# Attention scores of a transformer block: the first key tile of each unit in 64-key tiles of the array, the second in 128-key tiles

## The chip, the cores and the metric

The kernel runs on one core of one Trainium2 chip. The metric is the device time of an execution in microseconds (us). The engines named below are TensorE (PE; its weight loads are PEld in the profile), VectorE (DVE), ScalarE (ACT), GpSimd (POOL) and SyncE (SP), which here only starts transfers.

## The reference

A conditioned transformer block in float32, added to its own input. `x` is 4 x 1024 x 512, `cond_256` is 4 x 128, there are 16 heads of 32 features, and the feed-forward part has 2048 hidden features.

```python
def _tc_rmsnorm(x, t, gw, gb, bw, bb):
    g = (t @ gw.T + gb)[:, None, :]
    b = (t @ bw.T + bb)[:, None, :]
    inv_rms = jax.lax.rsqrt(jnp.mean(x * x, axis=-1, keepdims=True) + EPS)
    return g * x * inv_rms + b

def _attention(x, Wq, Wk, Wv, Wo):
    ...
    attn = jnp.einsum('blhd,bmhd->bhlm', q, k) / scale
    p = jax.nn.softmax(attn, axis=-1)
    o = jnp.einsum('bhlm,bmhd->blhd', p, v).reshape(B, L, D)
    return o @ Wo.T

def _swiglu(x, gate_w, hid_w, out_w):
    return jax.nn.silu(x @ gate_w.T) * (x @ hid_w.T) @ out_w.T

h = x + _attention(_tc_rmsnorm(x, t, g1w, g1b, b1w, b1b), Wq, Wk, Wv, Wo)
x = x + h + _swiglu(_tc_rmsnorm(h, t, g2w, g2b, b2w, b2b), gate_w, hid_w, out_w)
```

## The kernel before

Everything is kept with features on the 128 partitions and tokens in the columns. The 4096 tokens are 8 blocks of 512 (`NBLK`); a sequence is two blocks.

**Attention.** Its work is cut into `NR` = 256 units, numbered `r`. A unit is one block, one group of four heads (`HG`; 4 x 32 features fill the partitions), one half of 256 queries (`HQ`) and 256 of the 1024 keys, which are two key tiles of 128. Four units in a row (`UN`) go through all keys of one set of queries, called `j`. For a unit, `scores` (L307) takes keys as weights and queries as the moving data, one matmul for each head and key tile. A head's 32 features lie on 32 partitions, so each of these matmuls uses 32 rows of the array and 128 columns: the profile writes that as 32*128, and four heads are four tiles of the array that don't share rows. The result `sc` fills four of the eight PSUM banks, one bank for each head (two key tiles of 256 columns each), and there is one such buffer (`ps_sc`, L59). `keep` (L321) has ScalarE copy it to `raw` in SBUF. `running_max` takes the greatest score on VectorE; after the fourth unit `max_T`, `parts`, `parts_T` and `spread` turn the maximum into a shift for each query, laid out for all keys. `shifted` adds it on VectorE, `exponential` is ScalarE's, `weighted` (L374) multiplies the values by it on TensorE into `av`, and `accumulate` adds the exponentials of the four units with an accumulating DMA that GpSimd starts. `sums`, `inverse` and `normalize` finish a `j`.

**All other matmuls.** They go through `mm` (L109), which cuts a matmul's 128 output features into pieces of `columns[0]`: 32 in most of the program, giving 128*32 tiles, four of which share all rows and differ in columns. Transposes of the maximum (`mt`, L337) are 128*128, and some projections that follow them in the program's first part are too. A float32 matmul shows in the trace as two records of the matmul and two of the weight load; this is so on every line named here but the transposes.

**Order.** One hand-written loop over `g` (L774) sets the order of all engines but SP; nothing is reordered afterwards. In step `g` TensorE does `scores(g)`, later in the step `weighted` of unit `g` - 6, and between them the work of the feed-forward part or, before step `FS` = 60, the projections to keys, queries and values. The feed-forward products (`pa`, `pb`: a form of Strassen's product for gate and hidden; `pc`: the output product) fill the rest of each step from step 60 on; after step 268 they are alone. At `kind` 1 (every fourth step) `parts_T` stands ahead of the scores and `spread` behind them; otherwise `weighted` follows the scores directly. The loads are pinned to steps by a table.

Of the kernel before, what the change touches and what calls it, by code (L numbers as in the profile page):

```python
# [17 lines left out]
P = 128  # L18
# [6 lines left out]
def tile_cond_transformer_block(  # L25
# [13 lines left out]
    nc = tc.nc  # L39
# [267 lines left out]
    def scores(r: int):  # L307

        j, u = divmod(r, UN)
        m, qh = divmod(j, NB // HQ)  # L310
        keys, queries = kq[m, 0, u], kq[m, 1, qh]
        sc = ps_sc.tile([P, HG, 2, HQ], F32, tag="sc", name=f"sc{r}")
        for k in range(2):
            for i in range(HG):
                rows = slice(i * DH, (i + 1) * DH)
                nc.tensor.matmul(  # L316
                    sc[:, i, k, :], keys[rows, k * P : (k + 1) * P], queries[rows, :], start=True, stop=True
                )
        state["sc", r] = sc

    def keep(r: int):  # L321
# [382 lines left out]
    with tc.manual_schedule(  # L704
# [69 lines left out]
        while g < END:  # L774
# [16 lines left out]
            if g < NR:  # L791
                scores(g)
# [225 lines left out]
```

## Time and profile before

| | |
|---|---|
| median of 3 runs | 2432.27 us (2431.27 to 2441.08) |
| profiled execution, its own time | 2435.25 us |
| its span, first to last instruction | 2433.4 us |
| granted TensorE clock | 0.998 of full |
| scores (L316), matmul records | 4096, in 256 units |
| first and last start of a score matmul | 50.3 and 2088.5 us |

In the profile a group of instructions is named by its line, engine and operation and by what it writes and reads (`sc<-q,k`). The number behind x is the count of records. "128*32" ahead of a shape is the tile of the array that a matmul uses, rows by columns. Matmuls overlap, so a group's busy time is the time in which at least one of its records was running, and the mean length of one is longer than what it adds. What a block of matmuls costs is best read as the distance from its first start to the first start of what follows.

### The profile page before, as it was taken

To read this page: it belongs to the slowest core of one execution; us is meant where nothing else is said; L and a number is where in the kernel's file an instruction comes from. 1 tells how busy PE (TensorE), PEld (TensorE's weight loads), DVE (VectorE), ACT (ScalarE), POOL (GpSimd) and SP (SyncE) were. 2 spreads that over 40 slices of the span, in tenths; PEclk is the share of its full clock that TensorE was granted. 3 is DMA by queue.
4 is the path that set the end of the run, shared out by engine and by line. 5 is a ranking of instruction groups with operands and counts; after the bars stand their busy time and mean duration, and the time that the engine had idled before them with its cause. 6 is when DMAs were issued, how large, how long until landed. Compare 5 with 4: busy or idle time off the path is not lost. (4 is left out here: it accounts for less than half of the span.)

```text
span 2433.4 us, 72676 instructions
## 1 busy us (share of the span) xinstructions
PE 2378.9 (98%) x32553; PEld 1131.6 (47%) x32553; DVE 1938.6 (80%) x2183; ACT 1412.7 (58%) x1495; POOL 172.4 (7%) x207
## 2 busy tenths in 40 slices
PE   8999999999999999999999999999999999999999
PEld 3333334345454544545454545454545454434444
DVE  2688988888799988998899979997999799833322
ACT  3677777766566656755576657665666576512110
POOL 0000000000000000000000000000000000000000
PEclk9999999999999999999999999999999999999999
DMA  6599999988889788989888888898888889853442
GB/s 216 167 302 262 263 247 248 224 223 228 199 203 218 193 229 204 215 210 231 196 210 217 223 200 211 208 232 211 200 206 214 218 202 216 198 143 118 144 129 71
DMA packets 185988, 501.79 MB, mean 206 GB/s; under 512 B 21319, under 2 KB 78663, under 8 KB 158286
## 3 DMA queue, kind: packets, MB, share of 16 engines
q0 software_dynamic: 28656, 208.68, 44.3%
q1 hardware_dynamic: 156734, 288.47, 35.4%
q8 instruction: 256, 4.19, 0.7%
q14 instruction: 54, 0.44, 0.1%
q10 hardware_dynamic: 288, 0.01, 0.0%
HBM read 246.44 MB, written 41.97 MB: 119 GB/s over the span
## 5 line engine op out<-in xcount | busy, mean ns | idle before, releaser
L369 DVE TENSOR_TENSOR raw<-raw,shift 128x2048 f32<-128x2048 f32 (+1 forms) x320 | 588.8, 1856 | 26.1 <-ACT shift L364 26.1
L323 ACT COPY raw<-sc 128x2048 f32<-128x2048 f32 x256 | 479.6, 1873 | 181.6 <-PE sc L316 123.0
L372 ACT ACTIVATE raw<-raw 128x2048 f32<-128x2048 f32 x256 | 491.0, 1918 | 149.8 <-DVE raw L369 147.3
L328 DVE TENSOR_TENSOR rmax<-rmax,raw 128x1024 f32<-128x1024 f32 x384 | 469.5, 1223 | 47.5 <-ACT raw L323 41.2
L112 PE MATMUL pc<-h,ow 128*32 128x512 f32 x4096 | 469.1, 595 | 3.0 <-DMA ow<-in_out_w 2.1
L396 POOL DMA_DIRECT2D raw<-raw x192 | 165.3, 861 | 1944.9 <-ACT raw L372 864.3
L316 PE MATMUL sc<-q,k 32*128 32x256 f32 x4096 | 293.3, 400 | 1.1 <-ACT raw L323 1.1
L382 PE MATMUL av<-raw,v 128*32 128x256 f32 x4096 | 271.9, 383 | 21.6 <-ACT raw L372 21.1
L112 PE MATMUL pa<-x,fa 128*32 128x256 f32 x4096 | 269.9, 381 | 3.7 <-DVE pa L530 2.7
L112 PE MATMUL pa<-sums,fw 128*32 128x256 f32 x4096 | 267.9, 379 | 0.0
L112 PEld LDWEIGHTS pc<-h,ow 128*32 128x32 f32 x4096 | 128.3, 110 | 247.7 <-issue 226.6
L316 PEld LDWEIGHTS sc<-q,k 32*128 32x128 f32 x4096 | 184.9, 184 | 117.5 <-issue 74.9
L112 PE MATMUL pkq<-y,wkq 128*32 128x512 f32 (+1 forms) x1664 | 231.4, 594 | 4.3 <-ACT y L202 4.1
L112 PEld LDWEIGHTS pa<-x,fa 128*32 128x32 f32 x4096 | 123.4, 109 | 120.7 <-DVE pa L530 21.1
L112 PEld LDWEIGHTS pa<-sums,fw 128*32 128x32 f32 x4096 | 133.0, 110 | 88.0
L382 PEld LDWEIGHTS av<-raw,v 128*32 128x32 f32 x4096 | 110.4, 109 | 134.9 <-ACT raw L372 50.8
L583 DVE SCALAR_TENSOR_TENSOR res<-pc,res 128x512 f32<-128x512 f32 x128 | 88.2, 689 | 73.3 <-PE pc L112 70.4
L562 ACT ACTIVATE t<-pa 128x512 f32<-128x512 f32 x128 | 78.3, 611 | 109.9 <-PE pa L112 109.6
L545 ACT COPY pb<-pa 128x256 f32<-128x256 f32 x128 | 46.2, 361 | 164.3 <-PE pa L112 163.0
L112 PE MATMUL pb<-x,fw 128*32 128x256 f32 x2048 | 134.0, 379 | 1.2 <-ACT pb L545 1.2
L112 PE MATMUL pa<-x,fw 128*32 128x256 f32 x2048 | 134.0, 379 | 0.0
L112 PE MATMUL pb<-sums,fa 128*32 128x256 f32 x2048 | 133.9, 379 | 0.0
(108 smaller groups left out, 2163.9 us busy)
## 6 DMA issues: line engine op xcount, KB each, us to landing
raw<-raw POOLq DMA_DIRECT2D x192, 1024.0 KB, 9.2
fw<-sw SPq DMA_DIRECT2D x128, 512.0 KB, 7.1
fa<-in_gh_w SPq DMA_DIRECT2D x128, 384.0 KB, 6.1
ow<-in_out_w SPq DMA_DIRECT2D x128, 256.0 KB, 3.2
wkq<-in_kq_w SPq DMA_DIRECT2D x32, 512.0 KB, 6.3
v<-vs SPq DMA_DIRECT2D x128, 128.0 KB, 6.0
k<-kqs SPq DMA_DIRECT2D x124, 128.0 KB, 7.3
kqs<-st SPq DMA_DIRECT2D x61, 256.0 KB, 9.2
```

The lines of the kernel that those rows point to most:

```text
L112: nc.tensor.matmul(dst[k : k + n, :], w[:, k : k + n], moving, start=start, stop=stop, skip_group_check=seeded)
L316: nc.tensor.matmul(sc[:, i, k, :], keys[rows, k * P : (k + 1) * P], queries[rows, :], start=True, stop=True)
L323: nc.scalar.copy(raw[r].rearrange("p k h q -> p h k q"), state.pop(("sc", r)))
L328: nc.vector.tensor_tensor(rmax[j], rmax[j], raw[r][:, k, :, :], ALU.max)
L369: nc.vector.tensor_tensor(t, t, s.unsqueeze(1).to_broadcast(list(t.shape)), ALU.add)
L372: nc.scalar.activation(raw[r], raw[r], AF.Exp)
L382: nc.tensor.matmul(av[j][i * DH : (i + 1) * DH, :], v[m, u][:, k, i * DH : (i + 1) * DH], raw[r][:, k, i, :], start=(kt == 0), stop=(kt == ...
L396: nc.gpsimd.dma_start(out=acc[j].rearrange("p k h q -> p (k h q)"), in_=raw[r].rearrange("p k h q -> p (k h q)"), accum_op=ALU.add,)
L545: nc.scalar.copy(bank_b[p][:, RIGHT], bank_a[p][:, RIGHT])
L562: nc.scalar.activation(state["t", p], bank_a[p], AF.Tanh, scale=0.5)
L583: nc.vector.scalar_tensor_tensor(r, pp, 0.5, r, ALU.mult, ALU.add)
```

## The change

For the first key tile of each unit (`k` = 0), each head's matmul over 128 keys becomes two over 64 keys each, one behind the other: the first 64 keys go to partitions 0 to 63 of the head's bank, the other 64 to partitions 64 to 127. Each uses a tile of 32 rows and 64 columns of the array. The second key tile (`k` = 1) stays as it was, in tiles of 32 rows and 128 columns. Values written, their places and everything behind them are the same.

```diff
@@ -313,9 +313,16 @@
         for k in range(2):
             for i in range(HG):
                 rows = slice(i * DH, (i + 1) * DH)
-                nc.tensor.matmul(
-                    sc[:, i, k, :], keys[rows, k * P : (k + 1) * P], queries[rows, :], start=True, stop=True
-                )
+
+                wide = P // 2 if k == 0 else P
+                for part in range(0, P, wide):
+                    nc.tensor.matmul(
+                        sc[part : part + wide, i, k, :],
+                        keys[rows, k * P + part : k * P + part + wide],
+                        queries[rows, :],
+                        start=True,
+                        stop=True,
+                    )
         state["sc", r] = sc
```

## The prediction

> **What bounds the kernel now.** I read the page's first table, then the groups of instructions, then TensorE's records of the changed line, then a stretch of the timeline.
>
> The page's busy times and groups (busy us, mean ns of one | idle before and what ended it):
>
> ```profile
> PE 2378.9 (98%) x32553; PEld 1131.6 (47%) x32553; DVE 1938.6 (80%) x2183; ACT 1412.7 (58%) x1495; POOL 172.4 (7%) x207
> ...
> L323 ACT COPY raw<-sc 128x2048 f32<-128x2048 f32 x256 | 479.6, 1873 | 181.6 <-PE sc L316 123.0
> ...
> L316 PE MATMUL sc<-q,k 32*128 32x256 f32 x4096 | 293.3, 400 | 1.1 <-ACT raw L323 1.1
> L382 PE MATMUL av<-raw,v 128*32 128x256 f32 x4096 | 271.9, 383 | 21.6 <-ACT raw L372 21.1
> ```
>
> TensorE is busy 98% of the span; every other engine has room (VectorE 80%, ScalarE 58%). Only 54.5 us of the 2433.4 are free of matmuls. So time added to or taken from TensorE's stream of work moves the end almost one for one. The scores wait for nearly nothing (1.1 us in all 256 units). Their 2048 float32 matmuls appear as 4096 records: each is two passes over its 256 columns. Though scores and weighted values have equally many records of equal width, the scores take 293.3 us and the weighted values 271.9. The excess is the price of their other tiling (32*128, rows by columns of the array, amid 128*32), and the change is about nothing else.
>
> The records of the line (duration ns min/median/max):
>
> ```profile
> L316 PEld LDWEIGHTS sc<-q,k x4096: 181/184/185, 50.3 to 2088.3; 32*128 32x128 f32 x196
> L316 PE MATMUL sc<-q,k x4096: 374/374/478, 50.3 to 2088.5; 32*128 32x256 f32 x196
> ```
>
> Most records take 374 ns, the longest 478. In the trace these are the first four of a unit: they start with their own weight load and stand **104 ns** for it; later loads run behind matmuls.
>
> TensorE's timeline (start us, length us); compare starts, since ends are modelled and overlap:
>
> ```profile
> 1005.07 1.05 PE L112 MATMUL pa<-sums,fw 128*32 128x256 f32 x16
> 1005.93 1.05 PE L112 MATMUL pb<-sums,fa 128*32 128x256 f32 x16
> 1006.91 1.15 PE L316 MATMUL sc<-q,k 32*128 32x256 f32 x16
> 1007.99 1.07 PE L382 MATMUL av<-raw,v 128*32 128x256 f32 x16
> 1008.87 1.05 PE L112 MATMUL pa<-x,fa 128*32 128x256 f32 x16
> 1009.74 1.05 PE L112 MATMUL pa<-sums,fw 128*32 128x256 f32 x16
> 1010.60 0.61 PE L414 MATMUL sum<-raw,ones_sum 128*32 128x256 f32 x8
> 1011.14 1.09 PE L337 MATMUL mt<-ident,rmax 128*128 128x128 f32 x8
> ```
>
> Four things are to be seen. (1) Sixteen records inside one tiling take 1005.93 - 1005.07 = 0.86 us: four tiles at once, so four waves of **0.216 us**. (2) The same 16 records ahead of the scores take 0.98: changing the tiling costs **0.11 to 0.12 us**. (3) The scores last 1.08 from start to next start: 4 x 0.216 = 0.86, plus 0.104 for the exposed load, plus 0.11 for changing back. (4) From the sums to the transposes only the columns of the tile change, 32 to 128, with all rows kept, and it costs the same: 8 records, two waves or 0.43, take 1011.14 - 1010.60 = 0.54.
>
> **What the Trainium skill says.** "TensorEngine Tiling (Array Packing)", Key Properties: changing the tiling mode, not just the tile, drains TensorE. The trace agrees, at 0.11 us a time, also where only columns change. The same page, Available Configurations, lists 32x64 as eight independent tiles; no run here shows that mode. "TensorE: Matmul & The Clock Gate", LDWEIGHTS, says a load takes its columns divided by 1.2, in ns: 107 for 128, 53 for 64, 27 for 32. The trace agrees for 128 (104 exposed) and for 32 (the longest record of the weighted values is 404 against a median of 379: 25). The same page, Part 3, has 16 tiles split both ways running side by side; the trace of before has four at once, split one way.
>
> **The change part by part.** Per unit (there are 256):
>
> The first key tile was 4 matmuls of 32x128; it becomes 8 of 32x64, so 8 records become 16, each still 256 columns. They are 4 row groups by 2 halves. If all eight tiles run together, the array work stays two waves of 0.216: no gain, no loss. The weights hold the same number of columns.
>
> *Entering.* The stream still leaves 128*32, so that drain (0.11) stays. The exposed first load is of 64 columns: 53 ns by the skill, and 51 if I interpolate between the trace's 25 at 32 columns and 104 at 128. Saved: **-53**.
>
> *More starts.* Tiles start one after another, 7 ns apart in the records of the scores. Eight tiles end their starting 49 ns after the first instead of 21; the drain waits for the last. Added: **+28**.
>
> *The new switch in the middle.* Between the two key tiles the mode now goes from 32x64 to 32x128. I price it as in point 4, where only columns change: about 0.11 of drain. From the records' starts: the last start of one mode to the first of the next is 304 to 310 ns, against 196 within a mode, which makes **+112**. After it the first load of 128 columns has no matmul to hide behind, as now at entry: **+104**. This drain and this load did not exist, since the second tile's weights were loaded behind the first tile's matmuls.
>
> *Leaving.* From 32x128 to 128*32 as before: nothing.
>
> Sum: -53 + 28 + 112 + 104 = +191 ns a unit, times 256 = **+48.9 us**. The whole block, start to next start, goes from 1.08 to about 1.27 us.
>
> *What of it is hidden.* TensorE has waits that a later arrival would shorten: 21.1 us ahead of the weighted values (for ScalarE's exponential), 9 ahead of pa and 7 ahead of the sums where starts are later than in the undisturbed sequence. The waits ahead of weighted values number about 75 (by its weight loads), so at most 75 x 0.19 = 14 us can come back. But the copy of the scores, and the exponential queued behind it on ScalarE, also start later by what the scores lose, so I take about half or less: **-6**. Nothing else is reordered: no DMA, no wait and no buffer is added; the score banks are filled and emptied as before, ScalarE's copy waits 0.19 us longer and it has 42% idle. The program has 4096 more TensorE instructions (weights and matmuls, +6%); a unit's scores then have 24 record pairs in 1.27 us, 53 ns a pair, about the rate at which the whole stretch runs now (16 pairs in 0.86 is 54), so I price the issue at nothing. If this cover is gone, a first tile's 16 pairs at 54 ns take 0.86 instead of 0.43, +0.4 us a unit: the second rival below.
>
> Net +43 us. The profiled execution took 2435.25 us (span 2433.4, 1.85 around it), and the median of the runs is 2432.27, 3 lower. On the profile's time 2478, on the median **2475 us**.
>
> Bounds of what the trace does not show, the 32x64 mode: its drain may cost from 0 (the 64-to-128 change being no change of mode) to 0.12; its load exposed from 25 (no slower than 32 columns) to 104 (no faster than 128); the eight tiles from full overlap (0) to none between the halves (+0.43 a unit). The low end is a gain, hence the first rival.
>
> **The rivals.** *No drain in the middle (not slower).* Rows stay split by 32, and only the column limit moves; if TensorE lets the second tile's 128-column loads go into the background while the 64-wide matmuls run, the 112 and 104 fall away and -53 + 28 = -25 ns x 256 = -6 us: about 2426. The point that decides: if drain and exposed load in the middle are together under 72 ns instead of 216, a unit grows by less than 72 - 25 = 47 ns, and 256 x 47 ns = 12 us is the 0.5% named below. For it: the skill lists both as 4x row tilings. Against: the sums-to-transposes switch changes only columns and costs 0.11.
>
> *The halves don't overlap.* Both halves of a head lie in the same row group; in the program each matmul's two passes stand together. If a row group takes its work strictly in order, the second half's first pass starts only with the first half's second pass: one wave more, less the 28 of starts, so 191 + 188 = 379 ns x 256 = 97 us, less a little hidden: about 2525. If they don't overlap at all, two waves more: (191 - 28 + 432) x 256 = 152 us: about 2580. For it: no record of before has two tiles in one row group with split rows. Against: in 128*32 all four tiles share every row and run together, starting 3 to 7 ns apart.
>
> *The waits absorb it.* All 14 us of shortened waits come back, and a cheaper drain: +30, about 2462. This is the low side of my own case.
>
> **How the numbers follow.** Full overlap with a drain: 0.68, 2460 to 2490. Halves one wave apart: 0.11; not overlapping: 0.08. No drain: 0.11, within 0.5% but for a small part faster. A change of 0.5% (12 us) is about what a measurement of this kernel can tell from none. The range reaches from 2458 to 2540, through the one-wave rival; the no-drain and no-overlap ends, just under 2 in 10, are left out. Faster 0.04, same 0.09, slower 0.87.
>
> **What would show it.** The line of the scores should show 6144 records: 4096 of 32*64 with a longest of about 374 + 53 = 427 ns and 2048 of 32*128, whose first four a unit are still 478; weight loads near 135 ns for 64 columns. In the timeline the first key tile should last about 0.62 us, the second 0.64, the weighted values following at 1.27. A first tile of 0.83 or 1.03 means the halves wait for each other; a second one starting with 374 ns records means no drain. If the block grows by 0.19 us and the time by much less than 43, the waits ahead of the weighted values have shrunk; by much more, a queue behind the scores' copy has become late.

## The result and the profile after

The changed kernel takes 2465.01 us (median of 5 runs, 2464.53 to 2466.07) against 2433.89 before (5 runs): the ratio is 1.0121 with a 95% interval of 1.011 to 1.0132, so it is slower by about 31 us, clear of the spread of single runs (2431.27 to 2441.08 us before). The profiled execution took 2465.01 us with a span of 2463.2, 29.8 more than the span before, at the same granted clock of 0.998.

The page after, with the busy times and the groups of the scores, their copy and the weighted values (busy us, mean ns of one | idle before and what ended it; lines left out are marked):

```profile
PE 2421.6 (98%) x34601; PEld 1090.2 (44%) x34601; DVE 1940.6 (79%) x2183; ACT 1411.0 (57%) x1495; POOL 172.4 (7%) x207
...
L330 ACT COPY raw<-sc 128x2048 f32<-128x2048 f32 x256 | 479.6, 1873 | 210.7 <-PE sc L319 146.0
...
L319 PE MATMUL sc<-q,k 32*64 32x256 f32 (+1 forms) x6144 | 340.9, 409 | 0.2 <-ACT raw L330 0.2
...
L389 PE MATMUL av<-raw,v 128*32 128x256 f32 x4096 | 272.4, 384 | 15.3 <-ACT raw L379 15.0
```

TensorE is still at 98%, and VectorE and ScalarE are busy for the same time as before, to within 2 us. The scores' matmuls are busy for 47.6 us more (340.9 against 293.3). The span has grown by only 29.8 us, and one place where the difference went is in the last line: TensorE idles 15.0 us for ScalarE ahead of the weighted values, where it was 21.1.

The records of the scores' line after (duration ns min/median/max):

```profile
L319 PEld LDWEIGHTS sc<-q,k x6144: 127/131/185, 50.0 to 2122.4; 32*64 32x64 f32 x133, 32*128 32x128 f32 x66
L319 PE MATMUL sc<-q,k x6144: 373/400/479, 50.0 to 2122.6; 32*64 32x256 f32 x133, 32*128 32x256 f32 x66
```

The counts behind the forms are of a sample, two to one as they must be. In the single records, a weight load of 64 columns takes 127 to 133 ns. The first eight matmuls of a unit, of 64 columns, last 425 or 426 ns, 51 over the undisturbed 374; the first four of 128 columns last 478 or 479, as they did at the unit's entry before.

TensorE's timeline in the unit that was shown of before, unit 120 (start us, length us):

```profile
1021.39 1.05 PE L112 MATMUL pb<-sums,fa 128*32 128x256 f32 x16
1022.37 1.33 PE L319 MATMUL sc<-q,k 32*64 32x256 f32 x24
1023.63 1.07 PE L389 MATMUL av<-raw,v 128*32 128x256 f32 x16
1024.52 1.05 PE L112 MATMUL pa<-x,fa 128*32 128x256 f32 x16
```

The entry (1022.37 - 1021.39 = 0.98) and what follows are as before; the scores now last 1023.63 - 1022.37 = 1.26 us, and lasted 1.08. Inside them the single records have the first key tile for 617 ns from its first start to the first start of the second, and the second for 644 ns to the start of what follows. The first length holds in all 256 units to within 6 ns, the second wherever what follows doesn't wait. So the scores grew by 617 + 644 - 1076 = 185 ns a unit, 47.4 us in all; the span grew by 29.8.

### The profile page after: what moved, and what is told of

Its sections match the earlier page's. It is cut to its first block, busy times and chain, and to the rows that moved or that the text cites. A ratio compares the mean times of both kernels' runs of the same rounds, so it can differ in the third digit from the quotient of the medians.

```text
span 2463.2 us, 76771 instructions
## 1 busy us (share of the span) xinstructions
PE 2421.6 (98%) x34601; PEld 1090.2 (44%) x34601; DVE 1940.6 (79%) x2183; ACT 1411.0 (57%) x1495; POOL 172.4 (7%) x207
## 5 line engine op out<-in xcount | busy, mean ns | idle before, releaser
L319 PE MATMUL sc<-q,k 32*64 32x256 f32 (+1 forms) x6144 | 340.9, 409 | 0.2 <-ACT raw L330 0.2
L319 PEld LDWEIGHTS sc<-q,k 32*64 32x64 f32 (+1 forms) x6144 | 139.8, 147 | 209.3 <-issue 171.5
L371 ACT COPY shift<-sp 128x512 f32<-128x512 f32 x128 | 75.0, 586 | 106.5 <-PE sp L112 106.5
```

Source lines behind the costliest of these rows:

```text
L319: nc.tensor.matmul(sc[part : part + wide, i, k, :], keys[rows, k * P + part : k * P + part + wide], queries[rows, :], start=True, stop=True,)
L371: nc.scalar.copy(shift[j][:, k : k + 2, :], pp)
```

## Experiments

Two questions were tested. The first is what costs the 185 ns: a change of tiling in the middle of the unit ("switch"), the narrow matmuls themselves ("narrow"), or a drain in one direction only. The second is how TensorE's waits gave back the 17 us by which the span did not grow: each wait at most what its own unit had lost ("own unit only"), or also what several units before it had lost ("accumulating").

**No change of tiling within a unit: 64 keys in both key tiles.**

```diff
-                wide = P // 2 if k == 0 else P
+                wide = P // 2
```

(The lines marked - here and below are those of the changed kernel, so that the two read side by side. The times compared are always with the kernel before, run again beside each experiment.)

> Both key tiles of every unit in 64-key tiles of the array, so there is no change of tiling inside a unit. Theory 'switch': what the change costs is the change of tiling in the middle (drain 0.11 us and the exposed 128-column load 0.104 us). Without it only the shorter first load (-53 ns) and the longer row of starts (+26 ns) are left: the scores last 1.05 us from start to next start instead of 1.08 before the change, times 256 = -7 us; TensorE's waits grow back by 1 to 3 us of it, so 2428 to 2432 us, ratio 0.9975. Theory 'narrow': the 64-key matmuls themselves, twice as many instructions, are what costs; then twice as many cost twice as much: +60 us, 2495.

Measured: 2431.73 us against 2434.27, ratio 0.9989, interval 0.9981 to 0.9997. This is the only version that beats both kernels, if barely. Twice as many narrow matmuls as in the changed kernel cost nothing: "narrow" is out. The records of its scores:

```profile
L318 PE MATMUL sc<-q,k x8192: 374/374/426, 51.0 to 2087.8; 32*64 32x256 f32 x200
```

```profile
1006.25 1.05 PE L112 MATMUL pb<-sums,fa 128*32 128x256 f32 x16
1007.23 1.12 PE L318 MATMUL sc<-q,k 32*64 32x256 f32 x32
1008.28 1.07 PE L388 MATMUL av<-raw,v 128*32 128x256 f32 x16
```

No record is longer than 426, so no 128-column load stands exposed, and the timeline has the scores at 1.05 us as expected (1049 ns in the records, 27 less than before: 6.9 us). TensorE's waits between blocks of matmuls grew by 4.0 us, which leaves 2.9; the span shrank by 2.1. The second key tile is still there, and its first wave starts 216 ns after the wave before it, as within a key tile: going on to the second key tile costs nothing by itself.

**The two tilings in the other order.**

```diff
-                wide = P // 2 if k == 0 else P
+                wide = P if k == 0 else P // 2
```

> First key tile in 128-key tiles, second in 64-key tiles: one change of tiling in the middle, the other way round. Theory 'switch': the same sum in another order: entry with 0.104 us of exposed load, then a drain of 0.11 and 0.051 of exposed load, and the longer row of starts at the end: 1.26 us a unit, 2465 us as the changed kernel. Rival 'only towards wider': a drain is needed only when a tile grows over its neighbours' columns; going from 128 to 64 the second tile's loads go into the background and neither drain nor load shows: about 1.10 us a unit, 2438 us.

Measured: 2466.25 us, ratio 1.0131 (1.0118 to 1.0144), the changed kernel's time. The 128-key tile takes 644 ns and the 64-key tile 618, the same two lengths in the other order. So the switch costs the same towards narrower tiles as towards wider ones, and "only towards wider" is out.

**Three changes of tiling in each unit.** The first key tile in 64, the second in 128, for 128 queries at a time (lines that stay are left out at the marks):

```diff
-        for k in range(2):
-            for i in range(HG):
...
+        for q0 in range(0, HQ, P):
+            for k in range(2):
+                for i in range(HG):
...
+                            sc[part : part + wide, i, k, q0 : q0 + P],
...
+                            queries[rows, q0 : q0 + P],
```

> As the changed kernel, but done for 128 queries at a time: matmuls have half the columns, and a unit changes its tiling three times within itself instead of once. Theory 'switch': from start to next start 2 x (51 + 108 + 46 + 196) + 2 x (104 + 108 + 20 + 196) = 1658 ns a unit instead of 1076: +149 us before waits. For the waits: 'accumulating' (a wait gives back what TensorE lost over several units, up to the wait's whole length): of the 63.6 us of waits in the kernel before, of which 12 are in the first 100 us and 9 at the end, 25 to 32 are given back, so 2550 to 2558 us. 'Own unit only' (a wait gives back at most what its own unit lost): also up to some 30 here, because 0.58 us a unit is longer than most waits; so it doesn't tell those two apart, but the long waits do: the 1.27 us ahead of the weighted values once in 32 units should shrink to about 0.69 in both. Rival 'issue': 48 pairs of instructions in 1.66 us is 35 ns a pair; if TensorE can't be given them so fast, the waves come later than every 108 ns and the unit takes 2 us or more: 2640.

Measured: 2569.89 us, ratio 1.0559 (1.0545 to 1.0572). An undisturbed unit takes 404 + 433 + 404 + 433 = 1674 ns (1658 expected): +598 ns, 153.1 us. The span grew by 138.3. The time is 12 us over the range expected. Part of that is the unit, 16 ns longer than expected; in nine units the scores themselves stalled part of the way, 5.6 us together; and the waits gave back about 20 us (153.1 + 5.6 - 138.3) and not 25 to 32. The 1.27 us wait ahead of the weighted values, which both theories would have left at 0.69, is gone in the units where it stood. So neither theory of the waits is complete; why it went is open.

**All scores in 32-key tiles.**

```diff
-                wide = P // 2 if k == 0 else P
+                wide = DH
```

> All scores in 32-key tiles, 16 tiles at once, no change of tiling within a unit. Theory 'switch': first load exposed 25 ns instead of 104, row of starts 15 x 6.6 = 99 ns instead of 20: the two cancel: 241 + 3 x 216 ... from start to next start 241 + 216 + 216 + 99 + 304 = 1076 ns, as in the kernel before: 2434 us, within 3. Rival 'issue': 64 pairs of instructions for a unit's scores instead of 16; if TensorE's supply of instructions can't do it, waves start later than 216 ns apart or the blocks after the scores start late: over 2460.

Measured: 2570.22 us, ratio 1.0561 (1.0548 to 1.0575). "Switch" alone missed by 136 us; the time is where "issue" had it. TensorE's timeline and what it waited for (us in total, times, longest):

```profile
1007.17 1.49 PE L318 MATMUL sc<-q,k 32*32 32x256 f32 x64
1008.59 0.40 PE L112 MATMUL sp<-mT,select 128*32 128x256 bf16 x8
```

```profile
PE sc L318 <- issue: 23.0, 22, 2.0
PE pa L112 <- issue: 8.3, 9, 1.6
PE av L388 <- ACT raw L378: 6.7, 9, 1.3
PE av L388 <- issue: 6.4, 9, 1.2
```

The unit takes 1.42 us instead of 1.08, some 89 us in all; another 36 us are stalls in some of the units (last section). In the single records the first 32 matmuls start 7 ns apart, in two waves; then there is a hole of nearly 0.2 us, and most of the rest start 17 ns apart. The main wait is no longer another engine but "issue", time in which the engine waited for nothing that the profile shows. This fits a short supply of instructions, at 64 pairs of weight load and matmul in 1.42 us, but no run isolates it from other costs of the sixteen small tiles.

**The change in the odd units alone, and in the even units alone.**

```diff
-                wide = P // 2 if k == 0 else P
+                wide = P // 2 if k == 0 and r % 2 == 1 else P
```

> The change made in the odd units alone (128 of 256): 128 x 0.185 = 23.7 us are added to the scores. In the trace of the kernel before, TensorE's waits ahead of the weighted values stand in even units. 'Accumulating': a wait also gives back what the units before it lost, so about half of the 17 us come back here too, 6 to 9: 2449 to 2452 us, and in the first part of the program, up to unit 60, the long waits of the even units shrink by 0.19 to 0.25 us each. 'Own unit only': none of these waits shrinks, +23 us: 2457.

> The change made in the even units alone, 128 of 256, again 23.7 us added to the scores, now in the units that hold the waits. 'Accumulating': what odd and even units lose is nearly the same to a wait, so 8 to 11 us come back and the time is 2447 to 2450 us, within 3 us of the kernel with the odd units. 'Own unit only': all 17 us come back here, 2441 us, 15 us under that kernel.

Measured, against 2436.21 us: odd 2452.74 us, ratio 1.0069 (1.0054 to 1.0085), or +17 us; even 2446.67, ratio 1.0052 (1.0038 to 1.0065), or +13 us (the medians differ from before by 16.5 and 10.5). Both had 23.7 us added to the scores. "Own unit only" wanted +23 and +7; "accumulating" wanted the two within 3 us of each other. What came lies between: 4 to 6 us apart. The two intervals overlap a little, and the two profiled executions differ by more than the change (TensorE's clock was at half for about 3.4 us at three places after the start-up with the odd units, at none with the even ones), so single waits are a better witness than times and spans.

Unit 20 is even and has one of the waits. Its scores and weighted values, in the kernel before, the one with the odd units, the one with the even units, and the changed kernel, in this order (the last bracket is TensorE's idle time and what ended it):

```profile
202.92 1.15 PE L316 MATMUL sc<-q,k 32*128 32x256 f32 x16
204.66 1.07 PE L382 MATMUL av<-raw,v 128*32 128x256 f32 x16 [0.59 <-ACT raw L372]
```

```profile
205.75 1.15 PE L318 MATMUL sc<-q,k 32*128 32x256 f32 x16
207.30 1.07 PE L388 MATMUL av<-raw,v 128*32 128x256 f32 x16 [0.41 <-ACT raw L378]
```

```profile
204.14 1.33 PE L318 MATMUL sc<-q,k 32*64 32x256 f32 x24
205.80 1.07 PE L388 MATMUL av<-raw,v 128*32 128x256 f32 x16 [0.33 <-ACT raw L378]
```

```profile
206.78 1.33 PE L319 MATMUL sc<-q,k 32*64 32x256 f32 x24
208.26 1.07 PE L389 MATMUL av<-raw,v 128*32 128x256 f32 x16
```

From start to start: 1.74, 1.55, 1.66, 1.48. With only the odd units changed, unit 20's scores are as they were, and the wait behind them is shorter by 0.18 us all the same: what the odd units before it lost was given back here, which "own unit only" excludes. With all units changed, the weighted values start 0.66 - 0.21 = 0.45 us less late against an undisturbed unit: more than two units' worth from one wait. Unit 14's wait goes 1.64, 1.45, 1.45, 1.27 in the same order. In the feed-forward part both kinds of wait occur: at unit 92, and every 32 units after it, the wait of 1.27 us gives back only its own unit's 0.19, and nothing for the odd units; four units later, at 96, the waits together go from 0.82 to 0.63, 0.49 and 0.31.

Over all units but four with other disturbances (11, 12, 68 and 255), the waits ahead of the weighted values gave back 2.4 us with the odd units changed, 7.3 with the even ones and 9.4 with all. So both theories hold in part: the odd units alone should have given back nothing by "own unit only", and nearly as much as the even ones by "accumulating". Why the wait at 92 takes nothing from the units before it was not tested.

## Why the prediction was right, and which term was mis-sized

*The scores.* All four terms came out as priced. The eight narrow tiles run together: the second wave starts 267 ns after the first, 216 plus 51 of exposed load. The row of starts is 46 ns long instead of 20 (+26, taken as +28). The last start of the first key tile to the first of the second is 304 ns, 108 more than the 196 within a tiling (112 taken), and the second tile's first records stand 104 ns. The sum is 185 ns where the prediction had 191. Changing only the columns of the tile does drain TensorE, as the Trainium skill says of any change of mode ("TensorEngine Tiling (Array Packing)", Key Properties): 304 ns from last to first start, measured now from 64 to 128 and from 128 to 64.

*A loose reading.* The prediction called the 21.4 us of busy time between scores and weighted values the price of the scores' tiling. Busy time hides most of that price: by its own timeline the scores last 1.08 us and the weighted values 0.88, 0.20 us a unit or 51 us in all. No sum used the 21.4.

*The rivals.* "No drain" is refuted by the 304 ns; "the halves don't overlap" by the second wave at 267 ns, since with one more wave the first key tile would have taken about 0.83 us and not 0.617. "The waits absorb it" came nearest, with 2462 us, but half for the wrong reason: its drain was to be cheaper, and it was not. Issue costs next to nothing at 24 and at 32 pairs a unit (the kernel with all scores in 64-key tiles has 32 in 1.05 us, 33 ns a pair, and one stall of 0.4 us); at 64 pairs, 22 ns each, the unit is longer.

*What is hidden: the mis-sized term.* The prediction took 6 us of TensorE's waits as giving way, with a ceiling of 14 for those ahead of the weighted values, because each wait could give back at most its own unit's 0.19 us. Summed over all starts between blocks of matmuls that come later than in the undisturbed sequence, the waits went from 63.6 to 46.8 us: **16.8** came back, and 47.4 - 16.8 = 30.6 against the span's 29.8. Two things were wrong, as the distances between starts in both traces show.

First, the cap of one wait. Ahead of the weighted values 9.4 us came back. Of these, 6.5 us are within what each wait's own unit lost (65 waits, the prediction's term, taken as 6); 2.9 us are what twelve waits gave back beyond it, as at unit 20.

Second, and larger, the prediction named waits of 9 us ahead of `pa` and 7 us ahead of the sums, and then let nothing come back from them, without a reason. About 3.6 us came back ahead of `pa` and `pb`. Another 3.7 us came back at one place, the last `sum` of all. Before:

```profile
2146.11 1.05 PE L112 MATMUL pa<-sums,fw 128*32 128x256 f32 x16
2150.22 0.64 PE L414 MATMUL sum<-raw,ones_sum 128*32 128x256 f32 x8 [3.06 <-DVE raw L404]
2151.34 5.01 PE L112 MATMUL pc<-h,ow 128*32 128x512 f32 x32 [0.48 <-ACT total L419]
```

After:

```profile
2179.94 1.05 PE L112 MATMUL pa<-sums,fw 128*32 128x256 f32 x16
2181.69 0.64 PE L421 MATMUL sum<-raw,ones_sum 128*32 128x256 f32 x8 [0.71 <-PE pa L112]
2182.81 3.64 PE L112 MATMUL pc<-h,ow 128*32 128x512 f32 x32 [0.48 <-ACT total L426]
```

The wait is 2.3 us shorter, and the same 32 records behind it take 3.64 us instead of 5.01: before, the granted clock was 0.52 of full from 2150.6 to 2153.9 us, and after, it was 1.00 from 2182.8 to 2186.0. The wait for a transfer at unit 68 gave back nearly 1 us. Against that, 1.1 us went the other way at units 11 and 12, where the changed kernel's trace has its clock at half for about 3.4 us. The kernel with the two tilings swapped shows all these to within 0.1 us of the same size, so they seem to come with the added 185 ns a unit and not by chance of one execution. But they don't follow the time added in any simple way: in the kernel with all scores in 64-key tiles, which adds nothing, the wait ahead of the last `sum` is 1.8 us and not 3.1. How they come about was not followed up.

The predicted growth of 43 us became 31, with the sign, the mechanism and the size of every step on TensorE's own work right. That the time still fell into the range is owed to the width of the range and not to the term for the waits, which was almost 11 us too small.

## What to carry to other kernels

On an engine that is busy all the time, price a change of tiling as two costs, which appeared together here: the drain of the old tiling (108 ns) and the first weight load that nothing covers (104 ns for 128 columns, 51 for 64). It pays to look whether a block of matmuls can stay in one tiling: all scores in 128-key tiles and all in 64-key tiles are within 0.2% of each other here, and the mixture is 1.2% slower. When you work out how much of an added time is hidden, go through every wait of the bounding engine and not only the most frequent kind. Don't cap a wait at what its own round adds without looking: some waits here gave back what several rounds had lost, and others only their own round's part. And treat a long single wait apart: the last `sum`'s moved here by 1.3 us in a kernel that added no work.

## What the runs showed of the hardware that was not expected

The eight tiles ran as forecast, though the trace of before had no such tiles: in each of the four row groups two tiles with different columns run side by side, in both passes of a float32 matmul, and a wave of eight takes 216 ns, as a wave of four did.

With sixteen tiles the first two waves also held, but then starts came 17 ns apart instead of 7, after a hole of nearly 0.2 us. In that kernel 28 of the 256 units stalled inside their scores, by up to 2.6 us and 36 us in all. With three changes of tiling it was nine units and 5.6 us, with all scores in 64-key tiles one unit and 0.4 us, and in the changed kernel none. The stalls come with more instructions (the instruction queue moved 5.77 MB with the sixteen tiles and 4.19 MB before), but that this is their cause was not shown.

Behind the wait for the last `sum`, TensorE's granted clock was at half for about 3.4 us in the four traces where this wait was 1.3 to 3.1 us long (before, all 64-key tiles, three changes, odd units), and at full in the four where it was 0.6 to 1.0 us (after, swapped, 32-key tiles, even units). What sets the limit between them was not tested. Where the clock was at half behind it in the kernel before, 1.4 us were lost.
